# A graph layer's message sum: 544 chunks instead of 528 counted by source and type, first flush of 13 tiles, streamed blocks of five for six

## The chip, the cores and the metric

The kernel runs on one core of a Trainium2 chip. The metric is the device time of one launch in microseconds (us); less is better. The engines are TensorE (PE, with its weight loads PEld), VectorE (DVE), ScalarE (ACT), GpSimd (POOL) and SyncE (SP), which issues the plain DMAs. Each engine runs its own instructions in order.

## The reference

A layer of a graph network with four edge types. 12,500 nodes have rows `x` of 128 numbers; 200,000 edges, sorted by their target `dst`, have a source and a type.

```python
h = jnp.maximum(_layernorm(x, axis=-1), 0.0)
xs = h[src]
msgs = 0
for i in range(4):
    msgs = msgs + jnp.where((edge_type_4 == i)[:, None], xs @ W[i] + b[i], 0.0)
return x + jax.ops.segment_sum(msgs, dst, num_segments=12500)
```

Targets are drawn as the square of a uniform number, so the first nodes have very many edges each, and the last ones few.

## The kernel before

The edges stand in 1563 chunks of 128. The kernel treats them in two ways, and the constant `C0` (L56) is the border.

**Gathered chunks.** From chunk `C0` on, a chunk's 128 source rows of the normalized table `htab` are fetched with an indirect DMA from POOL (L544) into tiles `hm`, one DMA a chunk. DVE makes a one-hot of (type, target in a small window) for each chunk (L561), PE adds the rows up with three matmuls a chunk (L578; the table holds three bfloat16 parts of each float32), ACT copies the sums out (L581), PE multiplies them by the four weight matrices (L605) with the counts for the bias (L596, L603), and DVE adds the window of each chunk to `ring` (L666), a buffer of 16 tiles of 128 nodes that moves along the targets. Sixteen chunks are a *group*; the last groups have 12, 8, 4 and 3. The first three groups (48 chunks) are read from `x` itself before the table is ready (L528, L635). When all edges of some tiles have been added, those tiles *flush*: PE transposes them (L691), DVE adds `x` (L696), and SP writes them out. The first flush is of the first `NDT` tiles together, and it goes to a second buffer, `acc` (L708).

**Counted chunks.** For the chunks below `C0` the kernel counts how often each target has each (source, type), and multiplies the counts by the whole table. The first `ND` targets (those whose edges can lie in these chunks) get *slots* of at most 128 edges; the first target has 16 slots, most have one. For each slot DVE makes two one-hots, `o2` over 392 columns (L957) and `o1` over 128 (L961 or L965), and PE multiplies them (L983, 396 columns) into the counts of one *unit*. A unit packs three counts into one int32 with the factors 1, 256 and 65536, and holds one pair of light targets and one other, or three others. ACT casts a unit's counts to int32 (L989).

Up to `UB` = 27 units are a *batch*, and each batch is one *pass* over the table: 98 blocks of 128 table rows are streamed from HBM into tiles `hs` (L1029), and for each block PE makes three matmuls (L1033) whose moving operand are the unit bytes read as 8-bit floats (3 x 4 x 27 = 324 columns; the first batch is smaller). ACT copies the result out (`sd`, L1043), four matmuls with the weights follow (L1047), and DVE adds to `acc` (L1066). The stream has `STREAM` = 4 buffers of `HB` blocks each.

**What sets the order.** Before the dense work, a table stage normalizes `x` and writes `htab`, while the slots are built (L816 to L933) and the raw groups summed (L635). After that PE, DVE and ACT run an order written out by the program. `dense_work` (L1094) counts batch *n* + 1 while it multiplies batch *n*; the first batch is counted with no multiplication beside it, and the last multiplied with no counting. `count` (L938) makes sets of four slots, three sets ahead. The gathered groups are dealt in between by `pace` (L1079), which spreads them over the dense work by estimated columns; a slot of the first batch weighs 3.5 times its columns there (`alone_slot`). Dense work ends with group `FULL` - 1; the last five groups and the flushes come after it.

A DMA of the stream is issued by SP and waits until its buffer's last matmul is done. The pool `hpool` of gathered rows holds 11 tiles of two chunks.

Of the kernel before, what the change touches and what calls it, by code (L numbers as in the profile page):

```python
# [48 lines left out]
P = 128  # L49
# [3 lines left out]
SG = 4  # L53
WIN = 32
ROOM = 6
C0 = 528  # L56
UB = 27
MANY = 16
HB = 6
SLOTS = 4  # L60
SETS = 4
STREAM = 4
# [1 line left out]
RING = 2048  # L64
# [10 lines left out]
def kernel(  # L75
# [22 lines left out]
    assert NT * WIN == P  # L98
    DENSE = -(-C0 // P)
    E0 = C0 * P  # L100
    TM = T - C0
    BM = -(-TM // P)
    BR = 16
    BC = -(-TM // BR)
    assert C0 % 16 == 0 and C0 <= NFULL


    q = E0 / E
# [13 lines left out]
    def window_of(c):  # L122

        m = min((c - C0) // G, FULL)
        end = (C0 + (m + 1) * G if m < FULL else T) * P / E
        a_node = E * ((end**2 + 1 / N) ** 0.5 - end)
        return next((n for n in range(8, WIN, 2) if (n - 1) * a_node > P + 5 * P**0.5), WIN)

    NDT = -(-ND // P)
# [176 lines left out]
    def prep_steps(m, prep):  # L306
        c0, c1 = C0 + m * P, min(C0 + (m + 1) * P, T)
        got = []
        for name, of, rest in (("si", src, 0), ("ty", etype, NT), ("di", dst, N - 1)):
            t = prep.tile([P, 1, P], I32, name=name)  # L310
            edge_rows(t, of, c0, c1, rest)
            got.append(t)
        si, ty, di = got
        if c1 > NFULL and REST:
            r = (NFULL - c0) % P
            nc.sync.dma_start(di[r : r + 1, 0, REST:], dst[E - (P - REST) :].rearrange("(p e) -> p e", p=1))
        yield 0
        sf = prep.tile([P, 1, P], F32, name="sf")
        nc.vector.tensor_copy(sf, si)
        nc.vector.tensor_copy(head[:, m : m + 1], di[:, :, 0])  # L320
        rel = prep.tile([P, 1, P], F32, name="si")
        nc.vector.tensor_scalar(rel[:, 0, :], di[:, 0, :], head[:, m : m + 1], None, ALU.subtract)
        key = prep.tile([P, 1, P], F32, name="di")
        nc.vector.scalar_tensor_tensor(
            key[:, 0, :], ty[:, 0, :], span[:, m : m + 1], rel[:, 0, :], op0=ALU.mult, op1=ALU.add
        )
        nc.vector.tensor_reduce(ends[:, m : m + 1, 0], rel, AX.X, ALU.max)
        nc.vector.tensor_sub(ends[:, m : m + 1, 0], ends[:, m : m + 1, 0], span[:, m : m + 1])
        nc.vector.tensor_reduce(ends[:, m : m + 1, 1], rel, AX.X, ALU.min)
        yield 1  # L330
        pg = x_ps.tile([P, 2, P], F32, name="pt")
        nc.tensor.transpose(pg[:, 0, :], sf[:, 0, :], ident)
        nc.tensor.transpose(pg[:, 1, :], key[:, 0, :], ident)
        nc.scalar.copy(srcT[:, m % TURN, :], pg[:, 0, :])
        nc.scalar.copy(keyT[:, m % TURN, :], pg[:, 1, :])
# [368 lines left out]
    def put_out(j0, j1, again):  # L704

        c0 = j0 * P % RING
        n = (j1 - j0) * P
        rest = leave(j0, j1, ring, c0) if j0 else lambda: nc.vector.tensor_tensor(acc, acc, ring[:, :n], ALU.add)  # L708

        def end():  # L710
            rest()
            if again:
                nc.vector.memset(ring[:, c0 : c0 + n], 0.0)
            if c0 + n == RING:

                nc.vector.tensor_tensor(ring[:, :WIN], ring[:, :WIN], ring[:, RING:], ALU.add)
                if again:
                    nc.vector.memset(ring[:, RING:], 0.0)

        return end  # L720

    flushes = [(0, NDT, 0)]
    while flushes[-1][1] < NW:
        ja = flushes[-1][1]
        jb = min(ja + OT, NW, (ja * P // RING + 1) * RING // P)
        flushes.append((ja, jb, 0))
    assert NDT * P <= RING - 512

    def due(jb):

# [290 lines left out]
    def multiply(vs, counts):  # L1021
# [3 lines left out]
        pa = a_ps.tile([P, 512], F32, name="pa")  # L1025
        for j0 in range(0, NW, HB):
            j1 = min(j0 + HB, NW)
            hs = hsp.tile([P, HB, D3], BF16, name="hs")
            nc.sync.dma_start(hs[:, : j1 - j0, :], htab.rearrange("(p j) f -> p j f", j=NW)[:, j0:j1, :])  # L1029
# [49 lines left out]
    def pace(gi, part):  # L1079

        last = FULL - 1
        if gi >= last:
            return 2.0
        own = [columns(i) for i in range(LEAD, last)]
        a_group = (dense_columns() + sum(own)) / len(own)
        n = gi - LEAD
        if n < 0:
            return 0.0
        return ((n + part) * a_group - sum(own[:n]) - part * own[n]) / dense_columns()
# [214 lines left out]
    for gi, (t0, g) in list(enumerate(zip(starts, sizes)))[RAW:]:  # L1304
        q = (t0 + 8 * G) // P
        if (t0 + 8 * G) % P < G and 2 <= q < BM:
            steps = [prep_steps(q, later)]
        side = [lambda of=of: ending.append(put_out(*of)) for of in soon]
        for of in raw_adds[: RAW - 1 if gi == RAW else 1]:
            side += of  # L1310
        del raw_adds[: RAW - 1 if gi == RAW else 1]
        soon = list(flushing)
        flushing.clear()
        now = rows, oh
        if steps:
            side.append(lambda of=steps[0]: next(of, None))
        if gi < final:
            rows = gather(starts[gi + 1], sizes[gi + 1])
        parts = -(-g // HG)
        when = min(2, parts - 1)  # L1320
        todo = len(side) + G + 1 + (G if finish else 0)
        for j, part in enumerate(sum_up(t0, g, *now, gi >= FULL)):
            late, tails[:] = list(tails), []
            while work and spent < pace(gi, part):
                spent = next(work, None)
                if spent is None:
                    work = None
            for f in late:
                f()
            if checks and next(checks[0], None) is None:  # L1330
                checks.pop(0)
            if j == 0:
                if finish:
                    next(finish[0])
                if gi < final:
                    oh, made = one_hots_of(starts[gi + 1], sizes[gi + 1])
                    side += made
            if j == when:
                if finish:
                    next(finish.pop(0))  # L1340
                side.append(lambda: [ending.pop(0)() for _ in list(ending)])
                side += adds
                adds.clear()
                todo = min(todo, len(side) * parts // max(1, parts - 1 - j))
            left = todo * (parts - 1 - j) // parts - (0 if j >= when else todo - len(side))
            while side and len(side) > left:
                side.pop(0)()
            for _ in range(2):
                if leaving:
                    leaving.pop(0)()  # L1350
        assert not side
        if work is None and not dense_out:
            while tails:
                tails.pop(0)()
            for check in checks:
                for _ in check:
                    pass
            dense_out = True
            assert goes[0] < gi

            counting.close()
            leaves = [(ja, min(ja + OT, NDT)) for ja in range(0, NDT, OT)]
            late = [(ja, jb) for (ja, jb, _), i in zip(flushes, goes) if i >= gi]
            outp = mid.enter_context(tc.tile_pool(name="outs", bufs=len(leaves + late)))
            for ja, jb in leaves + late:
                seen_out[ja] = fetch(ja, jb)
            second = []
            for ja, jb in leaves:
                leaving.append(lambda ja=ja, jb=jb: second.append(leave(ja, jb, acc, ja * P)))
                if len(leaving) > 1:  # L1370
                    leaving.append(lambda: second.pop(0)())
            leaving.append(lambda: second.pop(0)())
        for (ja, jb, _), i in zip(flushes, goes):
            if i == gi < final - 1:
                flushing.append((ja, jb, True))
        if gi == final:
            for l in leaving:
                l()
            assert not ending and not flushing and not soon
            next(finish[0])  # L1380
            next(finish.pop(0))
            for ahead in (True, False):
                for (ja, jb, _), i in zip(flushes, goes):
                    if i >= final - 1 and (i < final) == ahead:
                        put_out(ja, jb, False)()
                for add in adds:
                    add()
                adds.clear()
        if gi == FULL - 3:
            assert q == BM - 1  # L1390
            check_chunks()
        if dense_out and not checked:
            checked = True
            check_all()
# [127 lines left out]
```

## Time and profile before

| | |
|---|---|
| median of three runs | 1647.18 us (1646.1 to 1649.81) |
| the profiled execution | 1651.06 us, span 1649.2 us |
| PE busy | 1457.4 us (88%) |
| DVE busy | 1041.5 us (63%) |
| POOL busy | 1011.6 us (61%) |
| ACT busy | 458.7 us (28%) |
| first multiplication L1033 | at 193.2 us |
| end of the first pass (`sd`) | 248.6 us |
| end of the last pass (`sd`) | 1594.7 us |

Matmuls overlap in the records: one takes some 300 ns from its start to its modelled end, but the next starts much earlier. What one costs in a row of equal ones is the distance from start to start. The busy time of a window counts overlapping stretches once.

### The profile page before, as it was taken

How to read it: one execution, taken by the hardware profiler on the slowest of the kernel's cores; microseconds unless marked ns; L12 is line 12 of the kernel's file. 1: busy time of each engine (PE TensorE's matmuls, PEld its weight loads, DVE VectorE, ACT ScalarE, POOL GpSimd, SP SyncE). 2: the span in 40 equal slices, each digit the busy share in tenths (PEclk: the TensorE clock that was granted, in tenths of full speed). 3: DMA queues.
4: the chain of work that ended last, by engine and by line, in shares of the span. 5: the costliest groups of instructions: out<-in, count | busy, mean ns of one | idle time of the engine just before them, and what ended most of it. 6: DMA issues, size and time to landing. Idle time of an engine off the chain costs nothing.

```text
span 1649.2 us, 33169 instructions
## 1 busy us (share of the span) xinstructions
PE 1457.4 (88%) x11293; PEld 958.5 (58%) x11293; DVE 1041.5 (63%) x5387; ACT 458.7 (28%) x1121; POOL 1011.6 (61%) x1062
## 2 busy tenths in 40 slices
PE   5678789999899999999999999999999999998975
PEld 2236476666566566666666666656565656565654
DVE  8792977666585766657576666657564756574333
ACT  6494222222222222222222222222222222222011
POOL 7435566666666666666666666666666566666562
PEclk9785799999999999999999999999999999999997
DMA  7452377766667766666666667666666566666652
GB/s 221 129 212 75 107 220 220 217 197 213 200 206 211 217 194 212 197 208 208 207 202 201 200 209 220 181 210 203 180 219 198 175 194 211 184 189 193 210 169 70
DMA packets 138411, 317.02 MB, mean 192 GB/s; under 512 B 25880, under 2 KB 78666, under 8 KB 138235
## 3 DMA queue, kind: packets, MB, share of 16 engines
q1 hardware_dynamic: 89323, 214.61, 41.7%
q0 software_dynamic: 48912, 100.24, 20.8%
q8 instruction: 89, 1.46, 0.4%
q14 instruction: 87, 0.71, 0.1%
HBM read 298.71 MB, written 16.04 MB: 191 GB/s over the span
## 4 chain that ended last, share of the span: by engine, by line
PE 81%; issue 8%; DVE 8%; ACT 2%; DMA 1%; DVEq 0%; SPq 0%; POOL 0%; ACTq 0%
PE pa L1033 47%; PE pt L983 12%; PE py L605 7%; PE ps L578 7%; DVE o L957 1%; PE pt L1047 1%; PE ps L635 1%; PE py L596 1%; PE pt L691 1%; DVE oh L561 1%; DVE o L965 1%; DVE ring L666 1%; PE pt L857 1%; DVE stt L440 1%; PE pt L854 0%
## 5 line engine op out<-in xcount | busy, mean ns | idle before, releaser
L544 POOL DMA_INDIRECT hm<-htab,srcT x987 | 954.7, 967 | 575.6 <-issue 226.0
L1033 PE MATMUL pa<-counts,hs 128*128 128x324 fp8e4 (+1 forms) x5586 | 1000.5, 304 | 50.2 <-issue 47.1
L1033 PEld LDWEIGHTS <-hs 128*128 128x128 bf16 x5586 | 519.0, 96 | 325.1 <-issue 84.7
L957 DVE TENSOR_SCALAR o<-iota_n,hkT 128x392 bf16<-128x392 f16 x1211 | 401.2, 331 | 75.4 <-PE pt L983 30.6
L983 PE MATMUL pt<-o,o 128*128 128x396 bf16 x1211 | 378.4, 336 | 37.0 <-DVE o L965 20.0
L989 ACT CAST counts<-pt 128x396 int32<-128x396 f32 x506 | 242.1, 493 | 500.5 <-PE pt L983 172.1
L561 DVE TENSOR_SCALAR oh<-iota_b,keyT 128x56 bf16<-128x56 bf16 (+8 forms) x987 | 167.7, 261 | 265.6 <-PE ps L578 94.6
L581 ACT COPY sb<-ps 128x224 f32<-128x224 f32 (+8 forms) x247 | 98.4, 399 | 480.3 <-PE pt L983 165.0
L578 PE MATMUL ps<-oh,hm 128*128 128x56 bf16 (+8 forms) x2961 | 189.1, 198 | 38.0 <-issue 35.3
L578 PEld LDWEIGHTS <-hm 128*128 128x128 bf16 x2961 | 163.0, 99 | 96.5 <-issue 49.1
L666 DVE TENSOR_TENSOR ring<-ring,py 128x14 f32 (+7 forms) x960 | 167.7, 175 | 65.0 <-PE pa L1033 13.0
L965 DVE TENSOR_SCALAR o<-iota,loT 128x128 bf16<-128x128 bf16 x660 | 178.4, 270 | 0.0
L983 PEld LDWEIGHTS <-o 128*128 128x128 bf16 x1211 | 114.8, 97 | 96.2 <-DVE o L965 27.4
L965 DVE TENSOR_SCALAR o<-iota,loT,byT 128x128 bf16<-128x128 bf16 x461 | 155.4, 337 | 0.0
L605 PE MATMUL py<-sb,wsb 128*128 128x224 f32 (+7 forms) x480 | 129.5, 412 | 1.3 <-issue 1.0
L605 PEld LDWEIGHTS py<-sb,wsb 128*128 128x128 f32 x480 | 88.2, 196 | 27.6 <-issue 5.6
L997 DVE COPY bi<-counts 128x27 int32<-128x27 int32 (+1 forms) x19 | 4.2, 220 | 113.3 <-issue 64.7
L528 POOL DMA_INDIRECT hx<-in_x_dram,srcT x48 | 51.3, 1069 | 35.9 <-DVE stt L440 22.4
L600 ACT CAST cnt<-py 128x224 bf16<-128x224 f32 (+7 forms) x60 | 23.7, 396 | 93.3 <-PE ps L578 29.9
L461 ACT ACTIVATE h<-hm,nmrt,rstdt 128x128 f32<-128x128 f32 x98 | 43.0, 493 | 1.0 <-DVE mvt L444 0.5
L1047 PE MATMUL pt<-sd,wsb 128*128 128x81 f32 (+1 forms) x152 | 25.8, 325 | 4.6 <-issue 4.6
L490 PE MATMUL ps<-h,ident 128*128 128x384 f32 (+1 forms) x34 | 16.3, 563 | 12.7 <-issue 11.6
(235 smaller groups left out, 666.6 us busy)
## 6 DMA issues: line engine op xcount, KB each, us to landing
hs<-htab SPq DMA_DIRECT2D x304, 576.0 KB
hm<-htab,srcT POOLq DMA_INDIRECT x987
htab<-h SPq DMA_DIRECT2D x32, 288.0 KB
xo<-in_x_dram SPq DMA_DIRECT2D x24, 256.0 KB
out_dram<-xo SPq DMA_DIRECT2D x24, 256.0 KB
hs<-htab SPq DMA_DIRECT2D x19, 192.0 KB
hm<-in_x_dram SPq DMA_DIRECT2D x18, 192.0 KB
hm<-in_x_dram SPq DMA_DIRECT2D x14, 168.0 KB
```

Of the source, the lines that this page charges most:

```text
L528: one = nc.gpsimd.indirect_dma_start(out=hm[:, i * D : (i + 1) * D], out_offset=None, in_=x, in_offset=bass.IndirectOffsetOnAxis(ap=srcf[: ...
L544: one = nc.gpsimd.indirect_dma_start(out=hm[:, (i - h0) * D3 : (i - h0 + 1) * D3], out_offset=None, in_=htab, in_offset=bass.IndirectOffse ...
L561: nc.vector.tensor_scalar(oh[:, i, :], iota_b[:, :K], keyf[:, at : at + 1], None, ALU.is_equal)
L578: nc.tensor.matmul(ps[:, i - i0, :], rows(i, c), oh[:, i, :], start=(c == 0), stop=(c == 2))
L581: nc.scalar.copy(sb[:, i0:i1].rearrange("p g t n -> p g (t n)"), ps[:, : i1 - i0, :])
L605: nc.tensor.matmul(py[:, :g, :], wsb[:, t, :], sb[:, :g, t, :], start=False, stop=(t == NT - 1))
L666: nc.vector.tensor_tensor(to, to, of(i), ALU.add)
L957: one = nc.vector.tensor_scalar(o2[:, k, :NB], iota_n, hkT[:, s : s + 1], None, ALU.is_equal)
L965: one = nc.vector.tensor_scalar(o1[:, k], iota_1, loT[:, s : s + 1], by, ALU.is_equal, ALU.mult)
L983: one = nc.tensor.matmul(pb, o1, o2, start=first, stop=last)
L989: nc.scalar.copy(counts[:, :, i * NT : (i + 1) * NT], pb.rearrange("p (b t) -> p b t", t=NT))
L1033: nc.tensor.matmul(pa[:, : 3 * nu * NT].rearrange("p (m v) -> p m v", m=3), hs[:, j - j0, c * D : (c + 1) * D], of, start=(j == 0 and c == 0),
```

## The change

```diff
-C0 = 528
+C0 = 544
 UB = 27
 MANY = 16
-HB = 6
+HB = 5
...
-    assert NDT * P <= RING - 512
+    assert NDT * P <= RING - 384
...
-            assert q == BM - 1
+            assert q >= BM - 1
```

Nothing else is written differently, but most numbers of the program are derived from `C0`:

| | before | after |
|---|---|---|
| counted chunks, gathered through `htab` | 528, 987 | 544, 971 |
| groups of 16 in the ordered part (and the four end groups) | 60 | 59 |
| targets with slots `ND`, tiles of the first flush `NDT` | 1480, 12 | 1568, 13 |
| slots counted | 1211 | 1255 |
| units, passes | 506, 19 | 535, 20 |
| first batch: units, slots | 20, 42 | 22, 66 |
| second batch: units, slots | 27, 62 | 27, 87 |
| matmuls L1033 | 294 of 240 columns, 5292 of 324 | 294 of 264, 5586 of 324 |
| stream loads, size of a full one | 323, 576 KB | 400, 480 KB |
| gathered groups done ahead of the first L1033, and of the second pass | 1.5, 3.88 | 2.25, 4.62 |
| slots counted ahead of the first L1033, and of the second pass | 52, 114 | 80, 163 |

The first batches have more slots because there are more pairs of light targets and so fewer units of three heavy ones: the heavy targets with two slots (targets 0 to 136) now come into the first two batches.

The order of DVE just before it starts on the second batch's one-hots (its first slots are those at L961; `oh` are a group's one-hots, `xo` the raw sums, `py` a group's sums). Before:

```order
L666 ISA
L666 TENSOR_TENSOR ring<-ring,xo 128x10
L561 TENSOR_SCALAR oh<-iota_b,keyT 128x48 x3
L957 TENSOR_SCALAR o_1779<-iota_n,hkT 128x392
L961 TENSOR_SCALAR o_2331<-iota_169,loT 128x128
```

After:

```order
L561 TENSOR_SCALAR oh<-iota_b,keyT 128x48 x6
L957 TENSOR_SCALAR o_1830<-iota_n,hkT 128x392
L965 TENSOR_SCALAR o_2473<-iota_169,loT,byT 128x128
...
L666 ISA
L666 TENSOR_TENSOR ring<-ring,py 128x10
L957 TENSOR_SCALAR o_1830<-iota_n,hkT 128x392
L961 TENSOR_SCALAR o_2604<-iota_169,loT 128x128
```

Before, the adds of the last raw group (`xo`) and 19 of the gathered groups' one-hots had been done by there. Now all raw adds, the 16 adds of the first gathered group (`py`) and 32 one-hots stand ahead of it, and 24 more slots.

The order of PE at the first multiplication. Before:

```order
L578 LDWEIGHTS hm
L578 MATMUL ps<-oh,hm 128x40
...
L983 LDWEIGHTS o_2345
L983 MATMUL pt<-o_1779,o_2345 128x396
L1033 LDWEIGHTS hs
L1033 MATMUL pa<-counts,hs 128x240
```

After:

```order
L596 MATMUL py<-oh,three 32x192
L578 LDWEIGHTS hm
L578 MATMUL ps<-oh,hm 128x48
...
L983 LDWEIGHTS o_2640
L983 MATMUL pt<-o_1830,o_2640 128x396
L1033 LDWEIGHTS hs
L1033 MATMUL pa<-counts,hs 128x264
```

Before, the first multiplication came in the middle of the second gathered group (40 columns); now that group is finished and the third (48 columns) begun.

The order of SP some passes in. Before:

```order
L677 DMA xo<-in_x_dram 128x4x128
L1029 DMA hs<-htab 128x2304 x12
L1029 DMA hs<-htab 128x768
L1029 DMA hs<-htab 128x2304 x16
L210 DMA si<-in_src_dram 128x128
```

After:

```order
L677 DMA xo<-in_x_dram 128x4x128
L1029 DMA hs<-htab 128x1920 x15
L1029 DMA hs<-htab 128x1152
L1029 DMA hs<-htab 128x1920 x9
L698 DMA out_dram<-xo 128x3x128
```

A pass was 16 loads of six blocks and one of two; it is now 19 of five and one of three. The first flush that goes out of the ring has three tiles for four.

## The prediction

> **What bounds the kernel now.** I read the page's chain first, then three stretches cut at the first multiplication, the end of the first pass and the end of the last.
>
> ```profile
> span 1649.2 us, 33169 instructions
> PE 1457.4 (88%) x11293; PEld 958.5 (58%) x11293; DVE 1041.5 (63%) x5387; ACT 458.7 (28%) x1121; POOL 1011.6 (61%) x1062
> ...
> PE 81%; issue 8%; DVE 8%; ACT 2%; DMA 1%; DVEq 0%; SPq 0%; POOL 0%; ACTq 0%
> L1033 PE MATMUL pa<-counts,hs x5586: 266/304/479, 193.2 to 1590.9; 128*128 128x324 fp8e4 x189, 128*128 128x240 fp8e4 x11
> L1043 ACT ACTIVATE sd<-pa x19: 378/440/447, 248.6 to 1594.7; 128x324 f32<-128x324 f32 x18, 128x240 f32<-128x240 f32 x1
> ...
> 160.00:190.00 30.00, 14.95 (x94) 6.86 (x95) 26.95 (x143) 9.34 (x24) 17.37 (x18) 0.59 0.29 78
> 193.00:248.60 55.60, 50.67 (x492) 40.75 (x490) 42.85 (x213) 15.17 (x38) 34.76 (x35) 0.97 0.69 215
> 248.60:1594.70 1346.10, 1240.05 (x9995) 819.99 (x9992) 834.38 (x4396) 321.24 (x769) 856.49 (x886) 0.99 0.66 202
> 1594.70:1649.20 54.50, 33.48 (x237) 25.29 (x237) 22.85 (x117) 7.72 (x18) 19.92 (x22) 0.73 0.35 99
> ```
>
> The columns of a stretch are its length, the busy time of PE, PEld, DVE, ACT and POOL, the granted clock, the DMA share and GB/s. So there are three regimes. While the first batch is counted alone (160 to 190), DVE is busy 26.95 of 30 us and PE half: **DVE sets that stage**. During the first pass (to 248.6) and the other 18 (1346.10 us, 74.8 each), PE is busy 91 and 92%: **PE sets the rest**, with POOL at 64% and the DMA engines at two thirds. What is PE's idle time there?
>
> ```profile
> PE pa L1033 <- issue: 47.1, 88, 3.9
> PEld L578 <- DMA hm<-htab,srcT: 3.7, 7, 0.9
> SPq L1029 <- PE ps L578: 352.8, 87, 11.0
> ```
>
> Mostly "issue", time in which it waits for nothing that shows; for gathered rows it waited 3.7 us in all. The stream's queue waits for PE to free buffers, not PE for the stream.
>
> **The change part by part.** Prices of PE first, start to start.
>
> ```profile
> 312.90 2.75 PE L1033 MATMUL pa<-counts,hs 128*128 128x324 fp8e4 x18
> 315.49 0.31 PE L578 MATMUL ps<-oh,hm 128*128 128x48 bf16 x6
> 315.64 1.45 PE L1033 MATMUL pa<-counts,hs 128*128 128x324 fp8e4 x9
> 316.93 0.83 PE L983 MATMUL pt<-o,o 128*128 128x396 bf16 x4
> 317.60 0.31 PE L578 MATMUL ps<-oh,hm 128*128 128x48 bf16 x6
> ...
> 239.68 1.49 PE L605 MATMUL py<-sb,wsb 128*128 128x192 f32 x8
> 241.00 0.31 PE L578 MATMUL ps<-oh,hm 128*128 128x48 bf16 x6
> 241.16 2.39 PE L1033 MATMUL pa<-counts,hs 128*128 128x240 fp8e4 x21
> 243.39 0.31 PE L578 MATMUL ps<-oh,hm 128*128 128x48 bf16 x6
> ...
> L1047 PE MATMUL pt<-sd,wsb 128*128 128x81 f32 (+1 forms) x152 | 25.8, 325 | 4.6 <-issue 4.6
> ```
>
> A matmul of 324 columns costs 2.59 / 18 = 0.144 us, one of 240 costs 2.23 / 21 = 0.106; linearly, one of 264 costs 0.117. A slot costs 0.67 / 4 = 0.168. A gathered group of narrow windows costs 8 x 0.15 (L578) + 1.32 (L605) and some 0.3 for L596 and L603, which I bound by two six-packs of L578: 2.8 us. The eight matmuls of L1047 cost 8 x 25.8 / 152 = 1.36 us.
>
> (a) *The steady passes, from the end of the first pass to the end of the last.* There are 19 for 18. One more pass is 294 x 0.144 = 42.3 us. Slots: 1255 - 163 = 1092 stand there for 1211 - 114 = 1097, -0.8. One more L1047 group: +1.4. Gathered groups: 58.0 - 4.62 = 53.4 for 59.0 - 3.88 = 55.1, so 1.74 fewer, all narrow: -4.9. Sum 38.0 us of PE. PE's idle time comes at its instructions all through the stretch, so I let it grow with the work: 1346.10 / 1240.05 = 1.086 gives **+41.2**. If none of it grew it would be 38.0; with a whole pass's share of idle, (1346.10 - 1240.05) / 18 = 5.9, it would be 43.9.
>
> The Trainium skill has another price for such a matmul: in "TensorE: Matmul & The Clock Gate", section "Back-to-back issue gap", it gives sustained streams of weight load and matmul as about 81 ns at 128 columns and 131 ns at 512, by which 324 columns would cost an estimated 107 ns and the pass 31 us. The rows above, 144 ns at 324 columns, are nearer that section's isolated gap (324 / 2.4 + 2.5 = 137.5 ns, an estimate by its formula), and the measurement decides.
>
> (b) *The first pass.* 294 x (0.117 - 0.106) = 3.2 us for the wider operand; 83 slots for 62 between its first and last matmul, 21 x 0.168 = 3.5; 2.37 groups for 2.38, nothing. 6.7 x 55.60 / 50.67 = **+7.4**. DVE has to make those 21 slots too, beside PE; its price follows.
>
> (c) *The first batch, counted alone.* Here DVE's prices count:
>
> ```profile
> 180.38 0.78 DVE L561 TENSOR_SCALAR oh<-iota_b,keyT 128x40 bf16<-128x40 bf16 x5
> 181.07 0.31 DVE L957 TENSOR_SCALAR o<-iota_n,hkT 128x392 bf16<-128x392 f16 x1
> 181.31 0.24 DVE L965 TENSOR_SCALAR o<-iota,loT 128x128 bf16<-128x128 bf16 x1
> 181.47 0.31 DVE L957 TENSOR_SCALAR o<-iota_n,hkT 128x392 bf16<-128x392 f16 x1
> 181.70 0.30 DVE L965 TENSOR_SCALAR o<-iota,loT,byT 128x128 bf16<-128x128 bf16 x1
> 181.92 0.31 DVE L957 TENSOR_SCALAR o<-iota_n,hkT 128x392 bf16<-128x392 f16 x1
> ...
> 183.40 2.49 DVE L666 TENSOR_TENSOR ring<-ring,xo 128x10 f32 x12 [0.31 <-DVE ring L666]
> 185.81 0.63 DVE L561 TENSOR_SCALAR oh<-iota_b,keyT 128x48 bf16<-128x48 bf16 x3
> ```
>
> Two slots take 181.92 - 181.07 = 0.85, so 0.425 each, two and a half times PE's price. The order has 80 slots for 52 ahead of the first multiplication: 28 x 0.425 = 11.9. It also has 16 adds more, 16 x 2.41 / 12 = 3.2, and 13 one-hots more, 13 x 0.69 / 5 = 1.8. DVE is full there, so all of it is path: **+16.9**. Those adds and one-hots, and 0.75 of a group on PE, are then missing later; PE's part is the one already taken off in (a). If PE's price held instead, the stage would grow by 28 x 0.168 = 4.7, at half the clock (0.59 was granted there) 9; these are the lower bounds.
>
> (d) *Building the slots.* ND passes 1536, so there is a fourth piece of 32 columns: 5 matmuls more at L825, 15 at L854 and L857, 10 more `sel` one-hots and a few masks, and 88 columns more in the wide operations.
>
> ```profile
> 84.69 0.40 DVE L816 TENSOR_SCALAR sel<-qa,cidx 128x136 f16<-128x136 f16 x2
> ...
> 91.28 0.46 PE L854 MATMUL pt<-sel,what 128*128 128x136 f16 x5
> 91.58 0.28 PE L857 MATMUL pt<-sel,what 128*128 128x136 f16 x2
> ```
>
> The nearest rows are the 136-column ones: 20 x 0.30 / 5 = 1.2 us on PE, and on DVE, two in 0.4 at most, 10 x 0.2 for `sel` and about as much for five masks and the widened rows, some 3. The two engines work side by side there, so it is between nothing (both covered by the table's own work) and 4.2 (one after the other); I take **+2.5**.
>
> (e) *Costed at nothing.* The 16 gathers fewer save POOL 16 x 954.7 / 987 = 15.5 us, which lies under PE's passes; the one preparation of edges fewer likewise. The 77 loads more are SP's, which waits for buffers anyway. At the end nothing is dealt differently: dense work again ends one full group before the last one of 16, and 12, 8, 4 and 3 follow. One tile leaves from `acc` instead of the ring, a transpose and a DMA each way; for the 54.5 us of the end I allow -1 to +2.
>
> ```profile
> L544 POOL DMA_INDIRECT hm<-htab,srcT x987 | 954.7, 967 | 575.6 <-issue 226.0
> ```
>
> The sum is 41.2 + 7.4 + 16.9 + 2.5 = **+68 us**. The profiled execution took 1651.06 us with a span of 1649.2; its span would become 1717. Against the median of the runs, 1647.18, I predict **1715 us**, 4.1% slower. A difference of 0.2%, 3.3 us, is about what a measurement of this kernel tells from no change.
>
> **The rivals.**
>
> *DVE bounds the first pass as well.* It was busy 42.85 of 55.60 us; 21 slots at 0.425 add 8.9. Less than the stretch would have (63 us), which speaks against it; for it, sets of four are wanted as a whole, so a late one stops PE. Then the first pass grows by 8.9 and a set's lateness at each of its 21 sets, at most 0.425 each: +17.8 for +7.4, 1725 us.
>
> *The five-block stream is late.* A steady pass takes 74.8 us for 98 blocks, 0.76 each; with one buffer in use, the other three covered 18 blocks, 13.7 us, and will cover 15, 11.4 us. A load of 480 KB at the 202 GB/s of the stretch takes 2.4 us. It decides only if landing takes over 11.4 us; if one load in ten were 1 us late, 40 us come on top, 1755. The queue's waits for PE speak against it. A rule of the Trainium skill does speak against smaller loads ("DMA: Bandwidth & Descriptors", section "Bandwidth": 1 MiB or more for three quarters of the peak rate); no run here shows a load of this size yet.
>
> *PE's matmul is not paced by its columns.* If a matmul of 324 columns could go at the price of one of 240, 0.106, the pass would cost 31.2: 11 us less, 1703. The 18 equal ones in a row above are against it.
>
> *Not slower: the gathers set the end.* A group cannot be added before its 16 rows are there. If POOL's 1.2 us a gather (967 ns and 226.0 / 987 of issue) paced the groups, 16 gathers fewer would take 19 us off, the pass would run inside PE's 106 us of idle time, and with (c) and (d) the kernel would end at 1647.2 + 16.9 + 2.5 - 19 = 1648. That point is where PE waits for `hm`; it waited 3.7 us.
>
> *The change does not do what it says.* The order has the 294 matmuls. What could still differ is the check of the ring's range (L768): the first flush leaves 384 of 2048 columns free where 512 were. If it failed, every chunk would be done again one by one, some thousands of us.
>
> **How the numbers follow.** Forecast 0.74; DVE bound in the first pass 0.14; stream late 0.05; matmul cheaper 0.03; gathers 0.03; slow path 0.01. The low end: no idle time growing (-3.2), 9 for 16.9 in (c) (-7.9) and nothing in (d) (-2.5) give 1701. The high end: DVE's rival (+10.4), (d) at 4.2 (+1.7) and the end at +2 give 1729, with a whole pass's share of idle (+2.7) 1732. Not all of these come together: range 1701 to 1730. Only the gathers' rival could be faster, half of it within 0.2%: faster 0.02, same 0.01, slower 0.97.
>
> **What would show it.** The first L1033 near 212 us for 193.2, DVE over 85% busy from 160 to there; the first `sd` near 275; 20 `sd` in all, the steady stretch near 1387 us with PE again 92% busy; 54 us from the last `sd` to the end. I am wrong if PE shows waits on `hs` or if its idle share in the passes moves by a point (14 us); if the steady stretch grows by far less than 38, the price of a matmul was not what its columns say.

## The result: no change where it was measured, and the profile after

| | before | after |
|---|---|---|
| median of 20 runs | 1648.12 us (1645.66 to 1654.17) | 1650.53 us (1639.24 to 1661.03) |
| ratio | 1 | 1.0008, 95% interval 0.9992 to 1.0024 |
| the profiled execution | 1651.06 us, span 1649.2 | 1661.03 us, span 1659.3 |

The forecast was 1715 us; the change cost nothing that can be measured. The head of the page of after, the first shares of its chain, and the rows of the lines that multiply and that end a pass (count; shortest, median and longest duration in ns; first and last start):

```profile
span 1659.3 us, 33991 instructions
PE 1500.5 (90%) x11597; PEld 991.3 (60%) x11597; DVE 1057.2 (64%) x5467; ACT 470.9 (28%) x1145; POOL 1000.1 (60%) x1046
...
PE 79%; DVE 8%; issue 4%; another core or an unknown queue 4%; ACT 3%; DMA 1%; DVEq 0%; SPq 0%; POOL 0%; ACTq 0%
L1033 PE MATMUL pa<-counts,hs x5880: 277/304/479, 216.4 to 1596.8; 128*128 128x324 fp8e4 x186, 128*128 128x264 fp8e4 x10
L1043 ACT ACTIVATE sd<-pa x20: 392/442/483, 276.0 to 1601.5; 128x324 f32<-128x324 f32 x19, 128x264 f32<-128x264 f32 x1
```

The 294 matmuls are there (5880 for 5586), and "issue" has fallen from 8% of the chain to 4%. The four stretches of after, cut as in the prediction (length; busy time and count of PE, PEld, DVE, ACT, POOL; granted clock; DMA share; GB/s), and the longest waits of PE in the steady one (total, times, longest):

```profile
0.00:216.40 216.40, 149.32 (x663) 80.58 (x664) 158.64 (x758) 118.10 (x307) 109.71 (x131) 0.74 0.43 134
216.40:276.00 59.60, 56.81 (x524) 42.61 (x523) 51.44 (x258) 15.33 (x38) 38.74 (x39) 1.00 0.71 210
276.00:1601.50 1325.50, 1262.53 (x10175) 843.44 (x10173) 824.35 (x4336) 329.80 (x785) 831.71 (x856) 0.99 0.70 210
1601.50:1659.30 57.80, 31.80 (x238) 24.69 (x238) 22.77 (x118) 7.67 (x18) 19.96 (x21) 0.72 0.33 93
...
PE pa L1033 <- issue: 12.9, 35, 1.1
PE pt L983 <- DVE o L965: 12.6, 8, 3.9
PE pt L983 <- issue: 9.7, 12, 3.9
```

Up to the end of the first pass the total came out as forecast: the first L1033 at 216.4 us (forecast 212), the first `sd` at 276.0 (275). One part was too small and the other too large, so the agreement of the second is partly luck; the table further down has both. DVE was busy 47.20 of the 56.40 us from 160 us to the first L1033, 84% where I had over 85. Then the 19 steady passes take 1325.50 us, where the 18 of before took 1346.10 and 1387 were forecast. PE's idle time there went from 106 us (1346.10 - 1240.05) to 63 (1325.50 - 1262.53) while its work grew. **More work took less time**, so the idle time was not a fixed share of the work.

The kernel before, timed again beside each set of runs, took about 1468 us in some sessions and 1648 to 1674 in others, so every ratio here is to the kernel before of the same session, and three single executions far outside (2027.82, 2894.43 and 3423.18 us, all in sessions of 1468) are left out. The results name the chip by a number only, and number 3 stands in sessions of both kinds; where the expectations say "a chip on which", read "a session in which".

### The profile page after: what moved, and what is told of

The parts are those of the page before. It is cut to its first block, busy times and chain, and to the rows that moved or that the text cites. A ratio compares the mean times of both kernels' runs of the same rounds, so it can differ in the third digit from the quotient of the medians.

```text
span 1659.3 us, 33991 instructions
## 1 busy us (share of the span) xinstructions
PE 1500.5 (90%) x11597; PEld 991.3 (60%) x11597; DVE 1057.2 (64%) x5467; ACT 470.9 (28%) x1145; POOL 1000.1 (60%) x1046
## 4 chain that ended last, share of the span: by engine, by line
PE 79%; DVE 8%; issue 4%; another core or an unknown queue 4%; ACT 3%; DMA 1%; DVEq 0%; SPq 0%; POOL 0%; ACTq 0%
PE pa L1033 47%; PE pt L983 11%; PE py L605 7%; PE ps L578 6%; DVE o L957 2%; DVE o L965 2%; PE pt L1047 1%; DVE ring L666 1%; PE ps L635 1%; PE pt L691 1%; PE py L596 1%; DVE oh L561 1%; ACT h L461 1%; DMA hm<-htab,srcT 1%
## 5 line engine op out<-in xcount | busy, mean ns | idle before, releaser
L544 POOL DMA_INDIRECT hm<-htab,srcT x971 | 945.1, 973 | 584.0 <-issue 214.8
L1033 PE MATMUL pa<-counts,hs 128*128 128x324 fp8e4 (+1 forms) x5880 | 1041.4, 304 | 21.6 <-issue 14.4
L1033 PEld LDWEIGHTS <-hs 128*128 128x128 bf16 x5880 | 548.9, 96 | 301.4 <-issue 38.1
L957 DVE TENSOR_SCALAR o<-iota_n,hkT 128x392 bf16<-128x392 f16 x1255 | 411.7, 328 | 56.9 <-PE pt L983 24.2
L983 PE MATMUL pt<-o,o 128*128 128x396 bf16 x1255 | 397.0, 342 | 44.6 <-DVE o L965 28.1
L989 ACT CAST counts<-pt 128x396 int32<-128x396 f32 x535 | 255.5, 494 | 539.4 <-PE pt L983 290.7
L578 PEld LDWEIGHTS <-hm 128*128 128x128 bf16 x2913 | 159.7, 99 | 80.0 <-issue 35.6
L578 PE MATMUL ps<-oh,hm 128*128 128x56 bf16 (+8 forms) x2913 | 183.0, 198 | 22.9 <-ACT sb L581 11.9
L983 PEld LDWEIGHTS <-o 128*128 128x128 bf16 x1255 | 119.5, 98 | 114.0 <-DVE o L965 37.3
L965 DVE TENSOR_SCALAR o<-iota,loT 128x128 bf16<-128x128 bf16 x690 | 185.9, 269 | 0.0
L965 DVE TENSOR_SCALAR o<-iota,loT,byT 128x128 bf16<-128x128 bf16 x505 | 167.6, 332 | 0.0
```

The costliest lines, as they stand in the source:

```text
L544: one = nc.gpsimd.indirect_dma_start(out=hm[:, (i - h0) * D3 : (i - h0 + 1) * D3], out_offset=None, in_=htab, in_offset=bass.IndirectOffse ...
L578: nc.tensor.matmul(ps[:, i - i0, :], rows(i, c), oh[:, i, :], start=(c == 0), stop=(c == 2))
L957: one = nc.vector.tensor_scalar(o2[:, k, :NB], iota_n, hkT[:, s : s + 1], None, ALU.is_equal)
L965: one = nc.vector.tensor_scalar(o1[:, k], iota_1, loT[:, s : s + 1], by, ALU.is_equal, ALU.mult)
L983: one = nc.tensor.matmul(pb, o1, o2, start=first, stop=last)
L989: nc.scalar.copy(counts[:, :, i * NT : (i + 1) * NT], pb.rearrange("p (b t) -> p b t", t=NT))
```

## Experiments: the size of the loads

The first theory (S) was that loads of five blocks for six made room for the pass. The kernel before (528 chunks) got loads of five, then of four, then of six in three buffers:

```diff
-HB = 6
+HB = 5
```
```diff
-HB = 6
+HB = 4
```
```diff
-STREAM = 4
+STREAM = 3
```

> The kernel before (528 counted chunks, 19 passes) with stream loads of five blocks for six; nothing else changes. Theory S (the load's size makes the gain: PE's idle gaps in the passes halve with five-block loads, whatever is counted): the changed kernel lost 27 us ahead of its second pass as forecast and its steady stretch was 62 us shorter than forecast, so here some 55 to 65 us come off, 1583 to 1593 us, and PE's gaps over 0.12 us in the steady stretch fall from 101 us to some 55. Theory W (the other make-up of the batches makes it, fewer slots and fewer gathered groups a pass): no change, 1645 to 1651 us.

> The kernel before with loads of four blocks (3072 bytes a partition for 4608), 16 blocks buffered for 24. If smaller loads are better step by step, it is faster than the one with five blocks by about as much again (some 1540 to 1570 us). If what matters is that a partition's piece lies under 4096 bytes (4608 before, 3840 with five), it is as the one with five, within 5 us of it. Theory W: 1645 to 1651 us, or slower if 16 blocks buffered cover a landing too little.

> The kernel before with six-block loads and three buffers for four: 18 blocks buffered, fewer than the 20 of five-block loads in four buffers, and the same 4608 bytes a partition. If the amount in flight or the room that the buffers take makes the gain, it is faster, 1583 to 1620 us. If the size of a load makes it (theory S), 1645 to 1651 us, or slower by PE's waits for late loads.

Measured in a session in which the kernel before took 1468.48 us: ratios 1.0006 (0.9997 to 1.0016), 1.0004 (0.9994 to 1.0014) and 1.0007 (0.9997 to 1.0016). The stream isn't late with 384 KB loads either. The Trainium skill prefers 1 MiB or more ("DMA: Bandwidth & Descriptors", section "Bandwidth"); all loads here are smaller, and 384, 480 and 576 KB made no difference where the stream isn't what is waited for. Theory S finds no idle time to take away here; its test where PE idles comes in the next section. The closest test, 544 chunks with loads of six in four buffers, does not fit: the buffers would take 18 KB of a partition, and 17.59 are left. Both S (1583 to 1593 us for five blocks) and the other theory of that text (1645 to 1651) missed. The surprise is the level, 180 us less than before with the same instructions. Stretches of the five-block version:

```profile
0.00:176.90 176.90, 129.06 (x574) 71.35 (x575) 140.79 (x665) 114.87 (x299) 101.54 (x121) 0.80 0.51 158
176.90:223.60 46.70, 46.23 (x483) 38.70 (x482) 41.44 (x208) 15.92 (x38) 34.75 (x35) 1.00 0.83 250
223.60:1423.00 1199.40, 1195.26 (x10000) 815.74 (x9999) 829.09 (x4401) 336.82 (x767) 861.28 (x885) 1.00 0.76 227
1423.00:1466.40 43.40, 29.32 (x244) 22.48 (x240) 22.64 (x117) 7.97 (x18) 21.11 (x23) 0.80 0.47 127
```

Here PE is busy 1195.26 of 1199.40 us. The same 10,000 matmuls counted 1240.05 us busy in the first trace: stops shorter than a matmul's record hide in its busy time, so of the 1346.10 us there 151 were stops, not 106. (The work itself was not slower: from start to start, one L1033 behind another took 143 ns in the median in both traces.)

## Experiments: the change again, and its sign turned

Theory P says that PE's work has a fixed price and the idle time is something apart; W, that the make-up of the dense work makes the idle time; G, that the gathers set the pace. Both kernels ran again unchanged, with 544 chunks in three buffers of six blocks, and 512 chunks in the kernel before:

```diff
-C0 = 528
+C0 = 544
-STREAM = 4
+STREAM = 3
```
```diff
-C0 = 528
+C0 = 512
```

> The kernel before, unchanged, for its trace on the chip on which 528 chunks with five, four and three buffers took 1468 us. Theory P (idle): PE has a fixed price of work, and what made 1648 us of it in the first measurement was PE's idle 'issue' time, 106 us of the steady stretch, and the work slowed by smaller pauses; here the steady stretch is 1199 us with PE over 99% busy, as in the runs with other buffers. Theory W (the make-up of the kernel makes the pauses): PE idles as in the first measurement, about 100 us in the steady stretch.

> The changed kernel, unchanged, on a chip on which PE has no pauses. Theory P: the forecast's terms hold where nothing pauses: steady passes +38 (no idle to grow), first pass +6.7, the first batch counted alone +16.9, slots +2.5, in all +64 for 1468, so 1532 us (1522 to 1542), PE over 99% busy in the steady stretch. Theory W (the change takes away what it costs, by its make-up): the ratio is 1.00 as in the first measurement, 1466 to 1474. Theory G (gathers set the end, 16 gathers fewer pay for the pass): 1466 to 1474 too, with waits of PE for hm.

> 544 chunks with loads of six blocks as before, in three buffers for four. Theory P: the size of a load is worth nothing, so within 3 us of the changed kernel, 1532. Theory S (smaller loads are what made room for the pass): slower than the changed kernel by 10 us or more.

> The kernel before with 512 chunks counted: 18 passes (17 of 27 units, the first of 17), 1003 gathers. Theory P: a pass and some of the first batch less than before, the change with its sign turned: about 1468 - 60 = 1408 (1398 to 1425), unless POOL, 1.2 us a gather (961.5 busy and 221 of issue for 987), then has 1201 us for what lies between the table and the end and holds PE up, up to 1440. Theory W: within 6 us of before. Theory G: 19 us slower than before, 1487.

The session was of the other kind: the kernel before took 1673.88 us, and 1672.43 in the one execution of `b528_again`. The changed kernel had ratio 1.0026 (1.0013 to 1.0038), three buffers of six 0.9990 (0.9972 to 1.0008), and 512 chunks **1.0121** (1.0098 to 1.0144). Loads of six blocks are, against S, if anything 0.4% quicker than five; there S falls. A pass less made the kernel slower, by 22 us (G had 19, W at most 6). The steady stretch of 528, of 544 and of 512 chunks:

```profile
247.00:1615.50 1368.50, 1246.54 (x9994) 822.23 (x9992) 831.17 (x4396) 321.24 (x769) 861.77 (x886) 0.99 0.66 198
```
```profile
275.50:1619.90 1344.40, 1268.11 (x10176) 845.10 (x10174) 823.55 (x4335) 327.93 (x785) 829.31 (x855) 0.99 0.68 207
```
```profile
241.00:1632.90 1391.90, 1226.12 (x9727) 793.61 (x9728) 820.04 (x4347) 311.75 (x747) 874.75 (x903) 0.98 0.63 189
```

The stretch grows as PE's work shrinks. What it follows is the last count, POOL's instructions, all but a few of them gathers: 1391.90 / 903 = 1.541 us each, 1368.50 / 886 = 1.545, 1344.40 / 855 = 1.572; in the first measurement 1346.10 / 886 = 1.519 and 1325.50 / 856 = 1.548. PE's busy time for each rises by 9% from 512 to 544 chunks (1226.12 / 903 = 1.358 us, 1268.11 / 855 = 1.483), the time by 2%. So the pace is not one fixed price: the changed kernel has 30 gathers fewer in this stretch, which at 1.519 us would take 45.6 us off; in the first measurement 20.6 came off, so some 25 of the pass's work still shows. Against P as I had put it, the price of a pass doesn't hold here; against G, PE waits for no gathered rows. How PE stops, in the timeline of the kernel before (start, duration, engine, line, tile, count, idle time ahead and who ended it):

```profile
845.59 0.99 POOL L544 DMA_INDIRECT hm<-htab,srcT  x1 [0.30 <-issue]
...
846.89 0.95 POOL L544 DMA_INDIRECT hm<-htab,srcT  x1 [0.31 <-issue]
...
847.61 0.24 PE L578 MATMUL ps<-oh,hm 128*128 128x72 bf16 x2
...
848.84 0.29 PE L578 MATMUL ps<-oh,hm 128*128 128x72 bf16 x4 [0.99 <-issue]
```

A chunk has three matmuls L578. PE stops for 0.99 us behind the second of them, when the rows must have been there for the first.

## Experiments: half the gathers

To part the gathers from the work, every second tile of gathered rows was left out; its matmuls read the tile before once more. The order on PE stayed the same:

```diff
         for h0 in range(0, g, HG):
+            if h0 % (2 * HG):
+                got.append(got[-1])
+                continue
             hm = hpool.tile([P, HG * D3], BF16, name="hm")
```

> The kernel before with every second tile of gathered rows left out: its matmuls read the tile before once more, so PE, DVE and ACT do the same instructions in the same order, with 494 gathers for 987. Theory G (the passes go at a fixed time for each gather, 1.52 to 1.57 us in the runs of 1650 to 1680 us, where PE could go faster): the steady passes fall from 1346..1369 us to what PE needs, 1200 to 1245 us as in the run of 1468 us; in all 1470 to 1530 us where the kernel before takes 1650 to 1675, and no change (within 5 us) where it takes 1468. Theory M (the make-up of the dense work, or PE's own instruction supply, makes PE's idle time): within 10 us of before on any chip.

> The same with the changed kernel: 486 gathers for 971. Theory G: with the gathers out of the way the change costs what its work on PE and DVE costs, the forecast's sum less the share of idle: +60 to +68 us over 528 chunks with half the gathers. Theory M: within 10 us of 528 chunks with half the gathers, as with all gathers.

> The changed kernel once more beside these two. Theory G: where the kernel before takes 1650 to 1675 us, ratio 0.998 to 1.005; where it takes 1468 us and PE never stops, +60 to +68 us, ratio 1.041 to 1.046. Theory M: ratio 0.998 to 1.005 on any chip.

The session was of the quick kind, 1468.12 us before. Half the gathers with 528 chunks: 0.9998 (0.9988 to 1.0007); with 544: 1.0439 (1.0421 to 1.0456), 64 us more. The changed kernel itself: 1535.19 us, ratio **1.0456** (1.0438 to 1.0473). Where PE doesn't stop, the change costs 67 us; 68 were forecast. Stretches of the changed kernel there:

```profile
0.00:194.70 194.70, 145.67 (x664) 79.55 (x665) 159.45 (x756) 117.98 (x306) 107.86 (x131) 0.76 0.48 149
194.70:251.50 56.80, 55.31 (x519) 42.09 (x518) 52.51 (x263) 15.59 (x39) 39.22 (x38) 1.00 0.75 219
251.50:1492.30 1240.80, 1232.89 (x10178) 838.71 (x10177) 820.04 (x4332) 346.04 (x784) 830.25 (x856) 1.00 0.75 224
1492.30:1535.40 43.10, 28.17 (x244) 21.98 (x241) 22.64 (x118) 7.88 (x18) 20.61 (x22) 0.84 0.47 130
```

Theory G (now for the long sessions alone) and M (the dense work or PE's own instruction supply) still needed a session of the other kind:

> 528 chunks with half the gathers once more, for a chip on which the kernel before takes 1650 to 1675 us (on one of 1468 us it made no difference, as theory G had it there). Theory G: there 1470 to 1530 us, steady passes 1200 to 1245 us, PE's issue idle in them below 30 us. Theory M: within 10 us of before, about 100 us of issue idle. Where before takes 1468 us: 1468 again by both.

> 544 chunks with half the gathers, beside it. Theory G: 60 to 68 us over 528 chunks with half the gathers on any chip. Theory M: where before takes 1650 to 1675 us, within 10 us of 528 chunks with half the gathers.

It came: the kernel before took 1649.56 us. Half the gathers with 528 chunks took **1482.33 us, ratio 0.8986** (0.8958 to 0.9014); with 544, 1555.90 (0.9432, 0.9399 to 0.9465), 74 us more (G had 60 to 68). The steady stretch of the first:

```profile
237.10:1436.90 1199.80, 1196.28 (x10000) 816.50 (x9999) 817.58 (x4400) 336.29 (x767) 427.87 (x444) 1.00 0.63 190
```

In the session of 1468 the same kernel had this row:

```profile
221.10:1420.80 1199.70, 1196.24 (x10001) 816.62 (x10000) 816.47 (x4399) 336.22 (x767) 428.12 (x444) 1.00 0.63 190
```

The two agree to 0.1 us. With half the gathers PE's stops in the passes are gone, and the two kinds of session with them. M falls. What stays longer is the part ahead of the first L1033, 191.0 us for 174.9, which holds the gathers of the raw groups; those weren't taken away.

## Experiments: bytes or number, wait or disturbance

Two kernels kept all 987 gathers and PE's order. One fetched only the first of a row's three parts (256 of 768 B), and all three matmuls read it:

```diff
-                    out=hm[:, (i - h0) * D3 : (i - h0 + 1) * D3],
+                    out=hm[:, (i - h0) * D3 : (i - h0) * D3 + D],
...
-                    in_=htab,
+                    in_=htab.rearrange("n (c d) -> (n c) d", d=D),
```

The other fetched one number a row, out of `x`, into small tiles that nobody reads, after a first full tile that all matmuls read:

```diff
+            if same:
+                few = fpool.tile([P, HG], F32, name="few")
...
-                    out=hm[:, (i - h0) * D3 : (i - h0 + 1) * D3],
+                    out=few[:, i - h0 : i - h0 + 1] if same else hm[:, (i - h0) * D3 : (i - h0 + 1) * D3],
...
-                    in_=htab,
+                    in_=x.rearrange("n (d o) -> (n d) o", o=1) if same else htab,
```

> 528 chunks, all 987 gathers, each of them fetching the first of a row's three parts (256 B of 768 B), which the matmuls of the other two read again: number of gathers, PE's, DVE's and ACT's instructions and their order as in the kernel before, a third of the gathered bytes. Theory B (what the gathers move sets their pace, and so the passes', where the kernel before takes 1650 to 1675 us): there 1470 to 1500 us, no idle of PE in the passes. Theory N (each gather costs POOL or its queue 1.52 to 1.57 us there, whatever it moves): within 10 us of before. Where before takes 1468 us, no change by both.

> 528 chunks, 987 gathers, but of one number a row (4 B) into small tiles that nobody reads; all matmuls read the first tile of gathered rows, so nothing of PE waits for a gather and no gather for PE. PE's order is that of before. Theory N, if the gathers' issue disturbs PE itself: idle of PE stays in the passes where before takes 1650 to 1675 us, at 1.5 us a gather; if only its buffers tie PE to the gathers: PE goes at its own pace, 1470 to 1490. Theory B: 1470 to 1490. Where before takes 1468 us: 1468.

> 512 chunks counted, 1003 gathers, all of the reference's work. Where before takes 1468 us (PE sets the passes): the change with its sign turned, 68 us less, 1400 (1395 to 1420), POOL at 1.25 us a gather still ahead. Where before takes 1650 to 1675 us (gathers set them): 16 gathers more at 1.54 us, +20 us as measured there before, ratio 1.010 to 1.014.

The session was one of 1468 us and told nothing on the first two, as both theories had it: 1468.88 and 1468.06 us. The profiled execution of 512 chunks took 1425.03 us beside 1468.35 of the kernel before, 43 us less. That is one execution without an interval, and less than the 48 to 73 us that I expected.

> A third of the gathered bytes with all 987 gathers, once more, for a chip on which the kernel before takes 1650 to 1675 us. Theory B: there 1470 to 1500 us, no idle of PE in the passes. Theory N: within 10 us of before. Where before takes 1468 us, no change by both, as measured.

> 987 gathers of 4 B a row that nobody reads, once more, for such a chip. Theory N, disturbed: idle of PE stays, within 10 us of before; tied by buffers alone: 1470 to 1490. Theory B: 1470 to 1490. Where before takes 1468 us: 1468, as measured.

> 512 chunks once more, for an interval. Theory N (gathers back to back leave PE and the others few instructions in some sessions): where before takes 1468 us, 1425 us as in the one undisturbed run, ratio 0.970; where before takes 1650 to 1675 us, slower by 1.0 to 1.4%.

Two sessions of the long kind followed. A third of the bytes: 1649.98 us, ratio 1.0014 (0.9997 to 1.0032), steady stretch 1347.30 us. So it is the number of gathers, not what they move. Its steady stretch, and POOL's gathers of 256 and of 4 B a row (busy us, mean ns; idle time ahead and what ended it):

```profile
246.80:1594.10 1347.30, 1240.08 (x9986) 820.63 (x9985) 831.03 (x4396) 321.43 (x768) 856.96 (x886) 0.99 0.55 158
```
```profile
L544 POOL DMA_INDIRECT hm<-htab,srcT x987 | 955.0, 968 | 576.7 <-issue 223.1 <-PE ps L578 127.2 <-PE pt L983 74.4
```
```profile
L550 POOL DMA_INDIRECT few<-in_x_dram,srcT x985 | 935.8, 950 | 1530.9 <-ACT keyT L336 1225.7 <-issue 296.1 <-ACT hx L462 8.1
```

The gathers of 4 B that nobody reads: **2704.28 us, ratio 1.640** (1.633 to 1.647). Theory N had the disturbance, but within 10 us of before: it missed the size by over 1000 us, and its price of 1.52 to 1.57 us a gather doesn't hold where POOL doesn't wait for PE's tiles. Behind the first tile nothing in that kernel makes a matmul wait for a gather. Two windows of it, one in which POOL gathers without a pause and one in which it doesn't gather:

```profile
600.00:640.00 40.00, 5.65 (x14) 1.57 (x15) 0.00 (x0) 0.49 (x1) 30.26 (x32) 0.50 0.07 15
...
800.00:840.00 40.00, 40.00 (x347) 27.73 (x346) 26.08 (x150) 11.00 (x28) 0.00 (x0) 1.00 0.49 151
```

The first window in the same kernel in the session of 1468 us:

```profile
600.00:640.00 40.00, 39.87 (x338) 27.59 (x337) 36.75 (x189) 10.95 (x25) 30.55 (x32) 1.00 0.55 166
```

With the same 32 gathers in 40 us, PE did 14 matmuls in the one session and 338 in the other; DVE did nothing at all, and 15 GB/s moved for 166. Whether DVE, ACT and the stream are held too, or wait for PE, these rows don't part. The granted clock of 0.50 in the first window doesn't explain it: at that clock a matmul's record takes 0.43 us for 0.30, and the pauses in the lines below are 1.67 and 2.37 us. The timeline shows it one by one (lines of this kernel are seven higher, L1040 is L1033):

```profile
910.37 0.43 PE L1040 MATMUL pa<-counts,hs 128*128 128x324 fp8e4 x1 [1.67 <-issue]
910.38 0.95 POOL L550 DMA_INDIRECT few<-in_x_dram,srcT  x1 [0.31 <-issue]
911.63 0.95 POOL L550 DMA_INDIRECT few<-in_x_dram,srcT  x1 [0.30 <-issue]
...
913.17 0.43 PE L1040 MATMUL pa<-counts,hs 128*128 128x324 fp8e4 x1 [2.37 <-issue]
```

Gathers come every 1.25 us, and PE gets in about one matmul in two of them. So in these sessions PE is disturbed by gathers in a row, and waits for none. Last, 512 chunks in a session of 1649.73 us: 1667.80 us, ratio 1.0115 (1.0086 to 1.0144), as G had it.

No version beats both kernels in both kinds of session: 512 chunks are quicker than both where PE sets the pace, by the one execution, and 1.2% slower where the gathers do.

## Why the prediction failed

| part, us | forecast | session of 1468 (528 with five blocks to 544) | first measurement |
|---|---|---|---|
| up to the first L1033, (c) and (d) | +19.4 | 176.9 to 194.7: +17.8 | 193.2 to 216.4: +23.2 |
| first pass, (b) | +7.4 | 46.7 to 56.8: +10.1 | 55.4 to 59.6: +4.2 |
| steady passes, (a) | +41.2 | 1199.4 to 1240.8: +41.4 | 1346.1 to 1325.5: **-20.6** |
| PE's busy time in them | +38.0 | 1195.26 to 1232.89: +37.6 | 1240.05 to 1262.53: +22.5 |
| behind the last `sd` | -1 to +2 | 43.4 to 43.1: -0.3 | 54.5 to 57.8: +3.3 |
| sum of the span | +68 | +69.0 | +10.1 |

The last column compares single profiled executions; by the medians the sum is +2.4. That the two sides cancel so nearly is luck: the steady passes gave back 20.6 us, and the parts ahead of them and behind took 30.7.

- **The step that failed** is in (a): "PE's idle time comes at its instructions all through the stretch, so I let it grow with the work". The trace gave those 106 us no cause ("issue"), and I took them for a share of the work. They belong to the gathers, and fell to 63. Counting the stops that hide in PE's busy time, 150.8 us of stops (1346.10 - 1195.26) became 92.6 (1325.50 - 1232.89): 58 us came back and paid for the pass's 37.6 and 20.6 more.
- The bounds of that step, 38.0 to 43.9, were one-sided: no reason excluded that idle time without a cause shrinks. Had it all gone, the stretch would have been 1240.05 + 38.0 = 1278 us for 1387, and the low end, which already had none of it growing, some 106 us lower.
- **The prices of the work were right.** PE's 37.6 for 38.0 shows it where PE never stops. The first pass took 2.7 us more than (b) had; PE's busy time rose by 9.1 there (46.23 to 55.31) for 6.7. The agreement of +41.4 with +41.2 is partly luck: 3.8 us of it are idle time (4.14 to 7.91), which are waits for DVE's one-hots `o` and not a share of the work. PE's waits in that stretch with 528 chunks in five blocks, and in the changed kernel in the session of 1468:

```profile
PE pt L983 <- DVE o L965: 3.5, 4, 2.7
```

```profile
PE pt L983 <- DVE o L965: 7.2, 9, 1.5
```

- **(e), "costed at nothing", held in one kind of session only.** I put the 16 gathers' 15.5 us under PE's passes. In the session of 1468 they lie there. In the others gathers cost PE time, whoever is busy.
- **The rival "the gathers set the end" had the right number**, 1648 us, and a chance of 0.03. It was weighed by a wrong sign: I said it decides "where PE waits for `hm`", and saw 3.7 us of that. The gathers act without such a wait, and at 1.52 to 1.57 us each in the passes, not 1.2; with another mechanism and another price, its number was partly luck.
- The stream of five blocks was never late, and "DVE bounds the first pass" took no more than the 2.7 us above.
- Of what I said would show me wrong, "if its idle share in the passes moves by a point" is what happened: from 7.9% to 4.8%.

The Trainium skill says in "SBUF — State Buffer", section "SBUF: two separate sides", that at its ports only DVE and GpSimd among the engines block each other and that PE never waits on anyone. By that rule gathers would cost PE nothing. The sessions of 1468 us agree (338 matmuls beside 32 gathers); those of 1650 don't (14). Either the rule has an exception there, or what holds PE lies elsewhere than in these ports; no run tells which.

**Open.** What differs between the sessions, and by what path a gather holds up PE, no run shows. Late instructions are not what the trace shows: in the steady stretch of the first measurement PE's matmuls start over 0.7 us apart 110 times, and only 13 of these stops overlap a packet of the instruction queues, no more than chance would give. Every gather moved 128 rows, so the number of gathers and the number of rows were not parted. That the real kernel settles at 1.52 to 1.57 us a gather because POOL has to wait for PE's tiles, and PE moves on meanwhile, is argued, not shown; how many gathers in a row PE can bear was not measured.

## What to carry to other kernels

Idle time to which the profile gives no cause has no known owner: let it run from nothing to all of it in the range, and find what it follows by changing one count at a time; here the passes followed the gathers, while PE was 88 to 95% busy. Take away half of a suspected disturber and leave the rest of the order as it is: that settled in one run what the waits in the trace could not name. Time the kernel before beside every experiment, since the same program differed by 12 to 14% from session to session, and a change cost 0% in one kind and 4.6% in the other.

## What the hardware showed that I had not expected

- One program, 1468 us in some sessions and 1648 to 1674 in others, each session within 0.7% but for the three single executions named above.
- In the long sessions indirect gathers 1.25 us apart leave PE 14 matmuls in 40 us for 338; with half the gathers of the kernel before PE loses nothing in the passes (1199.8 us for 1199.7).
- A gather of 128 rows costs POOL the same for 4, 256 or 768 B a row, about 0.95 us and 0.30 to the next, and a third of the bytes left the kernel's time as it was (1649.98 us for 1648.12).
- PE's busy time can hide stops: 1240.05 us and 1195.26 for the same 10,000 matmuls.
